# A four-layer decoder on one core: the last width attention and the int8 feed forward, run as two stages or woven into one

## The chip, the cores and the metric

The kernel runs on one core of one Trainium2 chip. The core has five engines that work side by side: TensorE (PE in the profile; its weight loads are shown apart as PEld), VectorE (DVE), ScalarE (ACT), GpSimd (POOL), and SyncE (SP), which here only issues DMAs. Each engine carries out its own instructions strictly in the order of its own program, and waits at a semaphore where it needs something from another engine. The metric is the time of one execution on the device in microseconds (us), the median of several runs.

## The reference, cut to what matters

The whole computation is a decoder of four layers of three blocks on `x`, 16 sequences of 128 tokens with 256 features. Each block's output is added to `x`, and the sum is layer-normed. Only the last two blocks of the twelve bear on this change:

```python
def _L3_xattn_ref(q, k, v, gamma):          # 8 heads; attention over the width
    ...
    qk = jnp.einsum('bhdq,bhdl->bhql', qh, kh) * scale
    sm = jax.nn.softmax(qk, axis=-1)
    ret = jnp.einsum('bhql,bhdl->bhdq', sm, vh)
    return gamma * ret.reshape(B, Dv, Lq)

def _L3_ffn_ref(x, W1, B1, W2, B2):
    X1_q, sX1 = quantize_rowwise(X1)        # round(x * 127/absmax of the row)
    W1_q, sW1 = quantize_global(W1)         # round(w * 127/absmax of the matrix)
    X2 = gelu(int8_matmul_dequant_bias(X1_q, W1_q.T, sX1, sW1, B1))
    X2_q, sX2 = quantize_rowwise(X2)
    W2_q, sW2 = quantize_global(W2)
    return int8_matmul_dequant_bias(X2_q, W2_q.T, sX2, sW2, B2)
...
x = _layernorm(x + _L3_xattn_ref(x, ctx_2048, ctx_2048, L3_xattn_gamma), axis=-1)
x = _layernorm(x + _L3_ffn_ref(x, L3_ffn_W1, L3_ffn_B1, L3_ffn_W2, L3_ffn_B2), axis=-1)
return x
```

Every operation of these two blocks works on one sequence at a time, apart from the two maxima over the whole weight matrices. So sequence 0 can be in the feed forward while sequence 4 is still in the attention.

## The kernel before, in words

The kernel holds all of `x` in SBUF as the tile `X` (128 tokens x 16 sequences x 256 features) and runs twelve stages, `s0` to `s11`, over it. Stages 0 to 2 are woven together; from stage 3 on, `run` opens the pools of one stage, traces it, and goes on to the next. The weights of stage n+1 are loaded (function `w11` for stage 11) when stage n begins. The last two stages are these.

**Stage 10, width attention.** `s10` calls `width_attention`, which stage 7 calls too. One `width_unit` is one sequence `b`. It is a generator: each `yield` ends a step. Its steps are: load `eo`, `e1` and `vp` by DMA (the profile prints `e1` as `e`); twice four matmuls of `eo` with `X` into four PSUM banks and four `tensor_reduce` on DVE that take the row maxima into `npad`; four transposes of `npad` and two DVE operations that make `xp`; twice eight matmuls of `e1` with `xp` and four Exp on ACT into `e`; twice eight matmuls of `vp` with `e`, and a copy on ACT into `o`; four transposes of `o`, two DVE reciprocals `rr`, two POOL multiplications into `rw`; four transposes of `rw`, one DVE product `y`, and two POOL additions of `y` to `X`. After every fourth sequence come two or three steps more (`finish_in_turns`): the layer norm of four sequences, whose statistics are made on DVE (`bn_stats`, `bn_aggr`), the power of -1/2 on POOL (`rsqrt`), and the normalisation on DVE; then 16 transposes on PE and two copies on ACT (`load_transposed`) that write `xT`, which stage 11 doesn't read.

The order of the work is written by hand. `rota(units, lags)` goes through turns n = 0, 1, 2, ...; in each it runs, for each lag in the list, one step of unit n - lag. `Ordered` then makes every engine keep this order: an instruction cannot be moved past another on PE, DVE, ACT or POOL. DMAs on SP stand outside this. The PSUM banks are two rings, six of `psA` (helper `ps`) and two of `psB` (helper `pt`); an instruction that writes a bank waits until the previous content of that place in the ring has been read.

**Stage 11, feed forward.** `s11` first quantises both weight matrices: a maximum on DVE, a maximum over the partitions on POOL (`partition_all_reduce`), then three DVE operations. Then it goes through the groups of four sequences: quantise `X` (`quantise`: maximum, reciprocal, two `tensor_scalar` that scale and round to a whole number in f32, then one `tensor_scalar` that takes the rounding constant off and writes bf16: `t11x` and `q11x`), transposes, the copy `xqT`; for each of the four sequences two matrix products into two banks, two DVE operations that scale and add the bias into `h`, one Gelu on ACT, again the quantisation (`am11h`, `s11h`, `t11h`, `q11h`), eight transposes, the copy `hqT`, eight matmuls, one DVE operation `y11`, one POOL addition to `X`. After each group come the layer norm of the four (`finish`) and one store of them. This stage isn't inside `Ordered`: the scheduler of the language places its instructions, and some of them stand between those of stage 10.

Of the kernel before, what the change touches and what calls it, by code (L numbers as in the profile page):

```python
# [12 lines left out]
F32 = mybir.dt.float32  # L13
# [7 lines left out]
NB = 16  # L21
S = 128
D = 256
# [303 lines left out]
class Decoder:  # L327
# [141 lines left out]
    def run(self):  # L469

        nc, tc = self.nc, self.tc
        names = list(self.stages)

        joint = names[:3] == [0, 1, 2]
        weights = self.weights = {}

        def side(n):
            return ("left", "right")[(n + (joint and n > 1)) % 2]

        def open_weights(n):  # L480
            cm = tc.tile_pool(name=f"w{n}", bufs=1, side=side(n))
            pool = cm.__enter__()
            weights[n] = (cm, getattr(self, f"w{n}")(pool))

        def close_weights(n):
            weights.pop(n)[0].__exit__(None, None, None)

        @contextmanager
        def pools(n):
            with (  # L490
                tc.tile_pool(name=f"k{n}", bufs=2, side=side(n)) as wk,
                tc.tile_pool(name=f"psA{n}", bufs=BANKS.get(n, (5, 3))[0], space=PSUM) as self.psA,
                tc.tile_pool(name=f"psB{n}", bufs=BANKS.get(n, (5, 3))[1], space=PSUM) as self.psB,
            ):
                yield wk

        open_weights(names[0])
        for j, n in enumerate(names):
            if joint and n in (1, 2):
                continue  # L500
            for m in names[1:3] if joint and n == 0 else names[j + 1 : j + 2]:
                open_weights(m)
            w = weights[n][1]
            with ExitStack() as later:
                if joint and n == 0:
                    k12 = later.enter_context(tc.tile_pool(name="k12", bufs=1, side="right"))
                with pools(n) as wk:
                    if j == 0:
                        for g in range(NG):
                            self.load_transposed(g)  # L510
                    if joint and n == 0:
                        held = self.s2_begin(k12, weights[2][1])
                        self.s0(wk, w, False, self.s12_early(k12, weights[1][1], held))
                    else:
                        getattr(self, f"s{n}")(wk, w, n == names[-1])
                close_weights(n)
                if joint and n == 0:
                    if len(names) > 3:
                        open_weights(names[3])
                    with (  # L520
                        tc.tile_pool(name="k2", bufs=2, side="left") as wk,
                        tc.tile_pool(name="psA2", bufs=5, space=PSUM) as self.psA,
                        tc.tile_pool(name="psB2", bufs=3, space=PSUM) as self.psB,
                    ):
                        self.s12_late(k12, wk, weights[1][1], held, len(names) == 3)
            if joint and n == 0:
                close_weights(2)
                close_weights(1)
# [1378 lines left out]
        return None  # L1907

    def s10(self, wk, w, last):
        self.width_attention(wk, self.row("s10_gamma"), last)  # L1910

    def width_attention(self, wk, gamma, last):
        nc = self.nc
        npad = [wk.tile([128, 512], F32, name=f"npad7_{n}", bufs=1) for n in range(3)]
        rw = [wk.tile([128, 2, 2, 128], F32, name=f"rw7_{n}", bufs=1) for n in range(3)]
        for t in npad + rw:
            nc.gpsimd.memset(t, 0.0)
        self.nc = Ordered(self.tc, nc)
        rota(
            [self.width_unit(wk, gamma, npad[b % 3], rw[b % 3], b, last) for b in range(NB)],  # L1920
# [1 line left out]
        )  # L1922
        self.nc = nc

    def width_unit(self, wk, gamma, npad, rw, b, last):
        nc = self.nc
        scale = 0.25
        eo = wk.tile([128, 2, D], F32, tag="eo7", name="eo7", bufs=3)
        e1 = wk.tile([128, 2, D], F32, tag="e17", name="e17", bufs=4)
        vp = wk.tile([128, 2, 8, 32], F32, tag="vp7", name="vp7", bufs=5)  # L1930
        cs = slice(b * 512, b * 512 + 512)
        nc.sync.dma_start(eo.rearrange("p r n -> p (r n)"), self.a["ctx_eo"][:, cs])
        nc.sync.dma_start(e1.rearrange("p r n -> p (r n)"), self.a["ctx_e1"][:, cs])
        nc.sync.dma_start(vp.rearrange("p k h d -> p (k h d)"), self.a["ctx_vp"][:, cs])
        yield
        xb = self.X[:, b, :]

        for mc in range(2):
# [11 lines left out]
        for r in range(2):  # L1950
            for mc in range(2):
                lo = 256 * r + 128 * mc
                nc.tensor.transpose(pm[:, r, mc, :], npad[:, lo : lo + 128], self.ident)
        xp = wk.tile([128, 2, D], F32, tag="xp7", name="xp7", bufs=3)
        for r in range(2):
            nc.vector.scalar_tensor_tensor(
                xp[:, r, :], xb, self.parity[:, r : r + 1],
                pm[:, r].rearrange("p m t -> p (m t)"), ALU.mult, ALU.add,
            )
        yield  # L1960
        e = wk.tile([128, 2, 4, 2, D], F32, tag="e7", name="e7", bufs=3)
        for n in range(2):
            banks = [self.ps(2, D) for _ in range(4)]
            for par in range(2):
# [8 lines left out]
        for par in range(2):  # L1973
# [4 lines left out]
                    )  # L1978
            if par == 0:
                yield  # L1980
        o = wk.tile([128, 2, D], F32, tag="o7", name="o7", bufs=3)
        nc.scalar.copy(o, p)
        yield
        p = self.pt(2, 2, 128)
# [16 lines left out]
        nc.vector.tensor_tensor(y, o, p.rearrange("p r m t -> p r (m t)"), ALU.mult)  # L2001
        for par in range(2):
            nc.gpsimd.tensor_tensor(xb, xb, y[:, par, :], ALU.add)
        if b % 4 == 3:
            yield
            yield from self.finish_in_turns(b // 4, last)

# [358 lines left out]
        nc.sync.dma_start(w["w2"], self.a["s11_w2"].rearrange("(c p) d -> p c d", p=128))  # L2366
        return w

    def s11(self, wk, w, last):
        nc = self.nc  # L2370
        wq, sw = {}, {}
        for n in ("w1", "w2"):
            src = w[n].rearrange("p a b -> p (a b)")
            am = wk.tile([128, 1], F32, name=f"am_{n}", bufs=1)
            nc.vector.tensor_reduce(am, src, AX.X, ALU.max, apply_absolute_value=True)
            al = wk.tile([128, 1], F32, name=f"al_{n}", bufs=1)
            nc.gpsimd.partition_all_reduce(al, am, 128, bass_isa.ReduceOp.max)
            s = wk.tile([128, 1], F32, name=f"s_{n}", bufs=1)
            nc.vector.reciprocal(s, al)
            nc.vector.tensor_scalar(s, s, 127.0, None, ALU.mult)  # L2380
            nc.vector.tensor_scalar(src, src, s, MAGIC, ALU.mult, ALU.add)
            q = wk.tile(list(w[n].shape), BF16, name=f"q_{n}", bufs=1)
            nc.vector.tensor_scalar(q, w[n], MAGIC, None, ALU.subtract)
            nc.vector.tensor_scalar(al, al, 1.0 / (127.0 * 127.0), None, ALU.mult)
            wq[n], sw[n] = q, al
        for g in range(NG):
            xq, am, _ = self.quantise(wk, self.X[:, 4 * g : 4 * g + 4, :], "11x")
            c1 = self.sm(4, tag="c111")
            nc.vector.tensor_scalar(c1, am, sw["w1"], None, ALU.mult)
            p = self.pt(2, 4, 128, dtype=BF16)  # L2390
            for j in range(4):
                for k in range(2):
                    nc.tensor.transpose(p[:, k, j, :], xq[:, j, 128 * k : 128 * k + 128], self.identb)
            xqT = wk.tile([128, 2, 4, 128], BF16, tag="xqT11", name="xqT11")
            nc.scalar.copy(xqT, p)
            for j in range(4):
                b = 4 * g + j
                h = wk.tile([128, 1, 1024], F32, tag="h11", name="h11")
                for n in range(2):
                    p = self.ps(512)  # L2400
                    for k in range(2):
                        self.mm(p, xqT[:, k, j, :], wq["w1"][:, k, 512 * n : 512 * n + 512], k, 2)
                    nc.vector.scalar_tensor_tensor(  # L2403
                        h[:, 0, 512 * n : 512 * n + 512], p, c1[:, j : j + 1],
                        self.row("s11_b1")[:, 512 * n : 512 * n + 512], ALU.mult, ALU.add,
                    )
                nc.scalar.activation(h, h, AF.Gelu_apprx_tanh)
                hq, am2, _ = self.quantise(wk, h, "11h")
                c2 = self.sm(1, tag="c211")
                nc.vector.tensor_scalar(c2, am2, sw["w2"], None, ALU.mult)  # L2410
                p = self.pt(8, 128, dtype=BF16)
                for k in range(8):
                    nc.tensor.transpose(p[:, k, :], hq[:, 0, 128 * k : 128 * k + 128], self.identb)
                hqT = wk.tile([128, 8, 128], BF16, tag="hqT11", name="hqT11")
                nc.scalar.copy(hqT, p)
                p = self.pt(D)
                for k in range(8):
                    self.mm(p, hqT[:, k, :], wq["w2"][:, k, :], k, 8)
                y = wk.tile([128, D], F32, tag="y11", name="y11")
                nc.vector.scalar_tensor_tensor(y, p, c2, self.row("s11_b2"), ALU.mult, ALU.add)  # L2420
                nc.gpsimd.tensor_tensor(self.X[:, b, :], self.X[:, b, :], y, ALU.add)
            self.finish(g, last)


def build(nc, arrays, at, stages):
# [15 lines left out]
```

## Time and profile before

| what | value |
|---|---|
| time, median of 3 runs | 4012.65 us (4009.0 to 4018.32) |
| time of the profiled execution | 4012.83 us |
| its span in the profile | 4011.1 us |
| first reduction of stage 10 (`npad`) on DVE | at 3705.72 us |
| last reduction of stage 10 | ends about 3853 us |
| first `h` of stage 11 on DVE | at 3885.56 us |
| last normalisation | starts at 4005.59 us, 1.38 us |
| DVE, PE, ACT, POOL busy over the whole span | 64%, 90%, 50%, 46% |

The span is counted from the first to the last instruction of the profiled execution; the 1.7 us between it and that execution's time lie outside. A profile line of a group of instructions reads: line of the kernel, engine, operation, what is written `<-` what is read, shapes, how often, then busy time in all and the mean of one in ns, then how long the engine sat idle just before them, and whom it waited for. L324 is the line in `Ordered` through which all the ordered instructions pass, so those are told apart by the names of their tiles. Shares over the whole span say little here: the change concerns the last 310 us.

### The profile page before, as it was taken

The page shows a single profiled execution, that of the slowest core. Times are in us where ns is not written, and L with a number is a line of the kernel's source. Part 1 is how long each engine was busy: PE and PEld are TensorE (multiplying, and loading weights), DVE is VectorE, ACT ScalarE, POOL GpSimd, SP SyncE. Part 2 cuts the span into 40 slices and gives each one's busy share as a digit, 9 for nine tenths or more (in the row PEclk, how much of TensorE's full clock was granted, in tenths as well). Part 3 has the DMA queues.
Part 4 walks back from the last instruction along what each step waited for, and adds up shares of the span by engine and source line. Part 5 has one row for each costly group of instructions (what it writes and reads, how often), then busy time and mean ns, then how long its engine had stood idle before and what let it go on. Part 6 is the DMA issues. An engine that isn't in the chain of part 4 may idle for free.

```text
span 4011.1 us, 96349 instructions
## 1 busy us (share of the span) xinstructions
PE 3606.3 (90%) x39250; PEld 2181.4 (54%) x39250; DVE 2572.9 (64%) x5611; ACT 2012.7 (50%) x4523; POOL 1829.3 (46%) x2013
## 2 busy tenths in 40 slices
PE   6999999999999738798989989888999999998975
PEld 4666666666665425574546655564454554554543
DVE  3776767768767565483245557656667666675786
ACT  2666666666666413352135535325565665664442
POOL 1444444435435227641145532216776666666221
PEclk7999999999999958899989989889999999999986
DMA  2111111111111001100100022101111111112200
GB/s 86 35 38 37 36 39 39 36 33 41 37 33 33 28 16 38 44 2 15 40 30 27 30 85 83 47 1 57 38 39 41 39 38 40 37 41 70 80 17 21
DMA packets 120649, 156.47 MB, mean 39 GB/s; under 512 B 15440, under 2 KB 79696, under 8 KB 119824
## 3 DMA queue, kind: packets, MB, share of 16 engines
q1 hardware_dynamic: 114352, 143.59, 11.5%
q8 instruction: 311, 5.10, 0.5%
q10 hardware_dynamic: 5712, 5.19, 0.4%
q0 software_dynamic: 144, 1.52, 0.1%
q14 instruction: 130, 1.06, 0.1%
HBM read 131.64 MB, written 2.10 MB: 33 GB/s over the span
## 4 chain that ended last, share of the span: by engine, by line
PE 76%; DVE 11%; ACT 5%; POOL 4%; issue 2%; DMA 1%; SPq 0%; ACTq 0%; POOLq 0%; DVEq 0%
PE bankA L324 40%; PE bankB L324 20%; PE bankC L324 8%; PE bankA L465 4%; PE bankB L465 4%; ACT accq L324 1%; DVE X L324 1%; ACT ot L324 1%; ACT gT L324 1%; POOL var L324 1%; DVE npad L324 1%; DVE accq L324 0%; POOL t L324 0%; DVE ln_st L324 0%; DVE h L2403 0%
## 5 line engine op out<-in xcount | busy, mean ns | idle before, releaser
L324 PE MATMUL bankA<-xT,wzx 128*128 128x512 f32 x1024 | 457.7, 600 | 0.0
L324 DVE SCALAR_TENSOR_TENSOR acc<-bankA,half,acc 128x508 f32<-128x508 f32 (+2 forms) x384 | 285.2, 743 | 166.8 <-ACT acc L324 157.8
L324 POOL TENSOR_TENSOR m<-m,gm 128x512 f32<-128x512 f32 x256 | 317.9, 1277 | 45.3 <-ACT m L324 45.3
L324 PEld LDWEIGHTS bankA<-xT,wzx 128*128 128x128 f32 x1024 | 189.8, 190 | 226.5 <-issue 188.3
L324 POOL TENSOR_TENSOR gT<-yx,sz 128x512 f32<-128x512 f32 x128 | 160.6, 1276 | 211.4 <-DVE yx L324 211.4
L324 PE MATMUL bankA<-xT,wkq 128*128 128x512 f32 x512 | 256.5, 625 | 0.0
L324 POOL TENSOR_TENSOR eb<-eb,c_tri_s 128x512 f32<-128x512 f32 x64 | 81.2, 1269 | 372.8 <-ACT eb L324 372.8
L324 PE MATMUL bankA<-xT,wvg 128*128 128x512 f32 x512 | 249.2, 609 | 0.1
L324 ACT ACTIVATE e<-bankA 128x512 f32<-128x512 f32 x320 | 165.2, 603 | 160.7 <-PE bankA L324 160.6
L324 DVE TENSOR_REDUCE npad<-bankA 128x2 f32<-128x512 f32 (+1 forms) x320 | 198.3, 683 | 59.1 <-PE bankA L324 58.8
L324 PE MATMUL bankC<-gT,wo 128*128 128x512 f32 x512 | 233.4, 599 | 2.7 <-POOL gT L324 2.7
L324 ACT ACTIVATE m<-bankA 128x512 f32<-128x512 f32 x256 | 132.1, 604 | 157.4 <-PE bankA L324 157.4
L324 POOL TENSOR_TENSOR sq<-sq,s 128x512 f32<-128x512 f32 x124 | 157.6, 1271 | 56.6 <-ACT s L324 51.9
L324 POOL TENSOR_SCALAR rs_ve<-o_mv 128x4 f32<-128x4 f32 x64 | 31.5, 492 | 299.0 <-DVE o_mv L324 289.7
L324 DVE SCALAR_TENSOR_TENSOR vT<-th,accv 128x512 f32<-128x512 f32 x64 | 45.3, 708 | 182.9 <-ACT th L324 182.9
L324 PEld LDWEIGHTS bankB<-y,tt 32*32 32x32 f32 x8192 | 86.7, 106 | 126.6 <-issue 90.2
L324 DVE SCALAR_TENSOR_TENSOR yx<-xs,cols,bankB 128x512 f32<-128x512 f32 x128 | 94.9, 747 | 90.2 <-PE bankB L324 84.5
L324 DVE SCALAR_TENSOR_TENSOR acck<-bankA,half_cols,acck 128x508 f32<-128x508 f32 (+2 forms) x192 | 142.5, 742 | 13.3 <-ACT acck L324 6.8
L324 PEld LDWEIGHTS bankC<-gT,wo 128*128 128x128 f32 x512 | 93.8, 192 | 99.3 <-issue 94.4
L324 DVE SCALAR_TENSOR_TENSOR accq<-bankA,half_cols,accq 128x508 f32<-128x508 f32 (+2 forms) x192 | 142.1, 740 | 4.5
L324 DVE SCALAR_TENSOR_TENSOR accv<-bankA,half_cols,accv 128x508 f32<-128x508 f32 (+2 forms) x192 | 140.0, 729 | 4.5
L324 ACT ACTIVATE m<-m 128x512 f32<-128x512 f32 x256 | 141.3, 650 | 0.0
(525 smaller groups left out, 9241.9 us busy)
## 6 DMA issues: line engine op xcount, KB each, us to landing
wzx<-in_s_wzx SPq DMA_DIRECT2D x64, 512.0 KB
up<-cums SPq DMA_DIRECT2D x1152, 2.0 KB
wkq<-in_s_w SPq DMA_DIRECT2D x64, 256.0 KB
wvg<-in_s_w SPq DMA_DIRECT2D x64, 256.0 KB
wo<-in_s_wo SPq DMA_DIRECT2D x64, 128.0 KB
sw<-qraw SPq DMA_DIRECT2D x64, 128.0 KB
eo<-in_ctx_eo SPq DMA_DIRECT2D x32, 256.0 KB
e<-in_ctx_e SPq DMA_DIRECT2D x32, 256.0 KB
```

The costliest lines, as they stand in the source:

```text
L324: return lambda *a, **k: self.tc.keep_in_program_order(f(*a, **k))
L465: self.nc.tensor.matmul(out, lhsT=lhsT, rhs=rhs, start=(k == 0), stop=(k == n - 1))
```

## The change

`s10` now traces both blocks. For each sequence there is a pair of generators: `width_unit` (A) without the layer norm at its end, and `s11_unit` (B), which starts with the layer norm of its sequence, does the feed forward of this one sequence, and ends with its second layer norm and the store of one sequence. `weave(units, order)` is the rota for pairs: in turn n each entry (A, lag) or (B, lag) runs one step of that generator of sequence n - lag. All of it is inside `Ordered`. `s11` does nothing more. Stages 0 to 9 issue the same instructions on every engine in the same order as before.

Besides, per sequence: the removal of the rounding constant (`q11x`, `q11h`), both factors `c111`, `c211` and both normalisations of `X` move from DVE to POOL; so does the last operation on the weights (`q_1`, `q_2`). The layer norms and the quantisation of `X` are done for one sequence at a time instead of four. The transposes into `xT` at the end of the attention are gone. `npad` and `rw` have one buffer each instead of three, and `eo`, `e1`, `vp`, `xp`, `e`, `o` have 2, 3, 4, 2, 2, 1 instead of 3, 4, 5, 3, 3, 3. The weights are quantised in four pieces (`first`), one at the start of the second step of each of the first four sequences. ACT now goes from Exp to Gelu and back in each turn in which both blocks are at work; the program has 25 table loads on ACT in this stage, where it had one.

```diff
     def s10(self, wk, w, last):
-        self.width_attention(wk, self.row("s10_gamma"), last)
+        if last:
+            return self.width_attention(wk, self.row("s10_gamma"), last)
+        nc = self.nc
+        npad, rw = self.width_zeros(wk, 1, 1)
+        _, w11 = self.weights[11]
+        with self.tc.tile_pool(name="kk11", bufs=2, side=self.side(11)) as wk11:
+            self.nc = Ordered(self.tc, nc)
+            first = self.s11_weights(wk11, w11)
+            units = [
+                (
+                    self.width_unit(
+                        wk, self.row("s10_gamma"), npad[b % len(npad)], rw[b % len(rw)], b, None,
+                        [2, 3, 4, 2, 2, 1], first,
+                    ),
+                    self.s11_unit(wk11, w11, b),
+                )
+                for b in range(NB)
+            ]
+            A, B = 0, 1
+            weave(units, [
+                (A, 1), (A, 4), (A, 0), (B, 9), (A, 1), (B, 6), (A, 3), (B, 9), (A, 3), (B, 7), (B, 5),
+                (A, 2), (A, 1), (B, 4), (A, 3), (B, 6), (B, 7), (B, 5), (A, 1), (B, 5), (B, 4),
+            ])
+            self.nc = nc
...
+    def s11_weights(self, wk, w):
...
+            nc.vector.tensor_reduce(am, flat, AX.X, ALU.max, apply_absolute_value=True)
+            al = w["s" + n] = wk.tile([128, 1], F32, name=f"al_{n}", bufs=1)
+            nc.gpsimd.partition_all_reduce(al, am, 128, bass_isa.ReduceOp.max)
+            yield
...
+            nc.vector.tensor_scalar(flat, flat, s, MAGIC, ALU.mult, ALU.add)
...
+            nc.gpsimd.tensor_scalar(q, src, MAGIC, None, ALU.subtract)
+            yield
...
+    def layernorm(self, b):
+        xb = self.X[:, b, :]
+        mv, rstd = self.moments([xb], 1e-5, "ln")
+        yield
+        self.nc.gpsimd.tensor_scalar(xb, xb, mv[:, 0, 0:1], rstd[:, 0:1], ALU.subtract, ALU.mult)
+
+    def quantise_row(self, wk, src, m, tag, bufs):
+        nc = self.nc
+        am, s = self.sm(1, tag="am" + tag), self.sm(1, tag="s" + tag)
+        nc.vector.tensor_reduce(am, src, AX.X, ALU.max, apply_absolute_value=True)
+        nc.vector.reciprocal(s, am)
+        nc.vector.tensor_scalar(s, s, 127.0, None, ALU.mult)
+        t = wk.tile([128, m], F32, tag="t" + tag, name="t" + tag)
+        nc.vector.tensor_scalar(t, src, s, MAGIC, ALU.mult, ALU.add)
+        q = wk.tile([128, m], BF16, tag="q" + tag, name="q" + tag, bufs=bufs)
+        nc.gpsimd.tensor_scalar(q, t, MAGIC, None, ALU.subtract)
+        return q, am
+
+    def s11_unit(self, wk, w, b, norm=True):
+        nc = self.nc
+        xb = self.X[:, b, :]
+        if norm:
+            yield from self.layernorm(b)
+            yield
+        xq, am = self.quantise_row(wk, xb, D, "11x", 1)
+        c1 = self.sm(1, tag="c111")
+        nc.gpsimd.tensor_scalar(c1, am, w["s1"], None, ALU.mult)
+        yield
+        p = self.pt(2, 128, dtype=BF16)
+        for k in range(2):
+            nc.tensor.transpose(p[:, k, :], xq[:, 128 * k : 128 * k + 128], self.identb)
+        xqT = wk.tile([128, 2, 128], BF16, tag="xqT11", name="xqT11", bufs=1)
+        nc.scalar.copy(xqT, p)
+        yield
+        h = wk.tile([128, 1024], F32, tag="h11", name="h11", bufs=2)
+        for n in range(2):
...
+            for k in range(2):
+                self.mm(p, xqT[:, k, :], w["q1"][:, k, cs], k, 2)
+            nc.vector.scalar_tensor_tensor(h[:, cs], p, c1, self.row("s11_b1")[:, cs], ALU.mult, ALU.add)
+        yield
+        nc.scalar.activation(h, h, AF.Gelu_apprx_tanh)
+        yield
+        hq, am2 = self.quantise_row(wk, h, 1024, "11h", 1)
+        c2 = self.sm(1, tag="c211")
+        nc.gpsimd.tensor_scalar(c2, am2, w["s2"], None, ALU.mult)
+        yield
+        p = self.pt(8, 128, dtype=BF16)
+        for k in range(8):
+            nc.tensor.transpose(p[:, k, :], hq[:, 128 * k : 128 * k + 128], self.identb)
...
+        nc.scalar.copy(hqT, p)
+        yield
+        p = self.pt(D)
+        for k in range(8):
+            self.mm(p, hqT[:, k, :], w["q2"][:, k, :], k, 8)
+        y = wk.tile([128, D], F32, tag="y11", name="y11")
+        nc.vector.scalar_tensor_tensor(y, p, c2, self.row("s11_b2"), ALU.mult, ALU.add)
+        nc.gpsimd.tensor_tensor(xb, xb, y, ALU.add)
+        yield
+        yield from self.layernorm(b)
+        nc.sync.dma_start(self.out[b], xb)
```

Written out, sequence b has its attention in turns b to b+4 (load; both halves of `npad`, `xp` and the first Exp; the second Exp; `o`, `rr`, `rw`; `y`), its first layer norm in turn b+4, `xqT` and `h` in b+5, Gelu and the quantisation of `h` in b+6, `hqT` and `y11` in b+7, and its last layer norm and the store in b+9. In a turn in which all sequences are there, DVE has in this order: four `npad`, `y`, statistics (of sequence n-9), four `npad`, the quantisation of `X` (n-5), two `xp`, statistics (n-4), two `rr`, the quantisation of `h` (n-6), `y11`, two `h`. POOL has: two additions of `y`, `rsqrt` and the normalisation (n-9), `q11x`, `rsqrt` (n-4), two `rw`, `q11h`, the addition of `y11`, the normalisation (n-4), and the two small factors.

## The prediction

> **What bounds the kernel now.** I read the table of stretches first, because the page's 90% for PE is a mean over twelve stages. Columns: busy us (and instructions) of PE, PEld, DVE, ACT, POOL, then the granted PE clock and the DMA share.
>
> ```profile
> 3740.00:3760.00 20.00, 20.00 (x218) 11.27 (x219) 15.63 (x30) 9.76 (x19) 6.00 (x9) 1.00 0.26 82
> ...
> 3880.00:3900.00 20.00, 9.24 (x44) 4.82 (x42) 19.78 (x43) 8.40 (x8) 0.72 (x1) 0.67 0.00 0
> 3900.00:3920.00 20.00, 13.82 (x63) 7.63 (x64) 15.94 (x46) 3.94 (x5) 4.14 (x5) 0.55 0.06 21
> 3920.00:3940.00 20.00, 9.99 (x58) 6.31 (x56) 16.47 (x39) 6.30 (x7) 2.93 (x3) 0.62 0.02 6
> ```
>
> Stage 10 (first line) has PE full at clock 1.00 and DVE at 78%. Stage 11 has DVE at 80 to 99%, PE half empty at clock 0.55 to 0.67, POOL nearly idle. From the first `npad` (3705.72) to the end (4011.1) pass 305.4 us. The groups of this part give what one sequence costs (busy us, then mean ns of one):
>
> ```profile
> L324 DVE TENSOR_REDUCE npad<-bankA 128x2 f32<-128x512 f32 x128 | 79.3, 683 | 20.1 <-PE bankA L324 20.1
> ...
> L2403 DVE SCALAR_TENSOR_TENSOR h<-bankA,c,rows 128x512 f32<-128x512 f32 x32 | 22.4, 743 | 0.0
> ...
> L2028 DVE TENSOR_REDUCE am11h<-h 128x1 f32<-128x1024 f32 x16 | 19.0, 1210 | 0.1
> ...
> L2034 DVE TENSOR_SCALAR t11h<-h,s11h 128x1024 f32<-128x1024 f32 x16 | 11.9, 744 | 0.0
> L2035 DVE TENSOR_SCALAR q11h<-t11h 128x1024 bf16<-128x1024 f32 x16 | 11.3, 707 | 0.0
> ```
>
> The reader is to see that the idle time before stage 11's DVE groups is nil: DVE sets its pace. In the timeline the first `npad` of successive sequences start at 3705.72, 3713.59, 3722.37, 3730.68 and 3739.82, so a turn of stage 10 takes 8.8 us.
>
> **The change, part by part.** The two stages have different bounds, so woven work can overlap; the question is what one turn with both blocks then costs on each engine.
>
> *DVE, one sequence.* Attention: two groups of four `npad` at 2.48 (timeline), two `xp` 0.87, two `rr` 0.28, `y` 0.69: 6.80. Feed forward: two times statistics (0.42 and 0.17) 1.18; `X` quantised: maximum 0.42 (stage 4's 128x256 reduction), reciprocal 0.15, scale 0.15, `t11x` 0.34; `h` quantised: 1.21, 0.15, 0.15, 0.74; `h` 2 x 0.74 = 1.48; `y11` 0.48: 6.45. Sum **13.25 us**. Gone to POOL are `q11h` 0.71, `q11x` 0.28, two factors and two normalisations at 0.41 to 0.43, some 2 us a sequence.
>
> *POOL.* Two additions 1.54; two `rsqrt` for one column each: 0.23 plus the power, 0.75 for two columns and 1.05 for four, so about 0.60 for one (estimate): 1.7; `rw` 1.18; addition of `y11` 0.72; two factors at 0.25. Two normalisations 128x256 with two operations: nearest row `od` at 1.15, so 2.3. The subtraction, one operation, is bounded by stage 5's `d`, shown below: 0.69 for 256 columns, 3.45 for 1280, so 2.7 ns a column: `q11x` 0.69, `q11h` 2.8. No row has POOL writing bf16, so `q11h` may lie between 2.8 and four times the 1.15 of `od`, 4.6; I take 2.8, the same operation. Sum **11.4** (13.2 with 4.6).
>
> *ACT.* Eight Exp (2.07 for four) 4.14, `o` 0.59, `xqT` 0.37, Gelu 1.06, `hqT` 1.01; two table loads at 1.28: 2.57. Sum **9.7**. The loads are priced by this place, where the next activation follows at once:
>
> ```profile
> 2691.38 1.06 ACT L2133 ACTIVATE parts<-parts 128x1024 f32<-128x1024 f32 x1 [3.54 <-DVE parts L2132]
> 2692.45 1.28 ACT L2134 ACT_TABLE_LOAD   x1
> 2693.74 1.06 ACT L2134 ACTIVATE parts<-parts 128x1024 f32<-128x1024 f32 x1
> ```
>
> The Trainium skill, page "ScalarE: Activation LUTs", section "What ACT_TABLE_LOAD costs", adds a drain of 1.38 us to each load, 2.66 us a switch, which speaks against a program that switches twice a turn; by it ACT would come to 12.5 us a turn. The three rows above show no such drain, since 0.01 us lies on either side.
>
> *PE.* The attention fills its 8.8 us at clock 1.00. The feed forward, from the timeline at clock 0.62: eight transposes 1.06, eight matmuls 1.89, four products 1.38 (5.52 for 16), two transposes 0.27: 4.6, so 2.9 at full clock. Sum **11.7** at clock 1.00, 13.4 if the feed forward's part stays slow.
>
> So DVE is the bound of a full turn. Three things come on top. First, DVE and POOL block each other (POOL's timeline, then DVE's, at the start of stage 5):
>
> ```profile
> 1834.73 3.45 POOL L1644 TENSOR_SCALAR d<-d5i 128x1280 f32<-128x1280 int32 x1 [3.33 <-PE bankB L324]
> 1838.16 2.19 POOL L1645 TENSOR_SCALAR d<-d5i 64x256 f32<-64x256 int32 x1
> ```
> ```profile
> 1836.61 3.05 DVE L1642 TENSOR_SCALAR gu<-gu5i 128x2816 f32<-128x2816 int32 x1
> ```
>
> `gu` ends at 1839.66; had it run from 1838.18, when the first `d` ended, it took 1.5; the second `d` then ran from 1839.66 to 1840.35, 0.69. Each stood still while the other ran. Other DVE work isn't touched: four `npad` take 2.48 beside POOL's additions (from 3748.59; POOL busy from 3747.95 to 3749.49) as they do alone (3743.97). In a full turn DVE has four `tensor_scalar` (`s11x`, `t11x`, `s11h`, `t11h`), and POOL is busy 11.4 of some 15 us. By program order the first two meet the end of a normalisation, the last two the two `rw` of 0.59: 0.1 + 0.6, I take **0.7**; the ends are 0 and 3.3 (each pair behind a normalisation, 1.15, and half an `rw`, 0.5). The Trainium skill, page "SBUF — State Buffer", section "Who interferes with whom", says that a DVE instruction with at most one SBUF input and no two-port mode doesn't contend; by it `npad`, `xp`, `y` and `h` stay free and only those four count. If all DVE work counted, the turn would be up to 13.25 + 11.4 = 24.7 us.
>
> Second, the last part of a turn is a chain over engines: `rr` frees the bank for the transposes of `q11x`, then `xqT`, then eight matmuls 1.15, four products 0.9, then `h`. From `rr` to `h` that is 0.2 + 0.5 + 1.2 + 0.9 = 2.8. Beside it DVE has the quantisation of `h` and `y11`, 2.73. So it is just covered; I take **0.3**, and 0 to 1 as its ends. Third, hand-overs and a PE clock below 1.00: PE with 11.7 of 15 us is like stage 8, where it is 84% busy at clock 0.87; its chain links grow by 0.15. I take **0.7**, between 0 and 1.5. Full turn: 13.25 + 0.7 + 0.3 + 0.7 = **15.0 us**, ends 13.3 and 17.8 (not all at their worst).
>
> *The sum.* Turns 1 to 4, attention alone: 34.1 as now (3739.82 - 3705.72), plus on DVE the second weight's maximum 2.28, both scalings 2 x 1.28 and small ones 0.3: 39.3. (The first maximum, 2.28, lies in DVE's idle time ahead of 3705.72; `q_1` and `q_2`, about 5.6 each by 2.7 ns a column, lie where POOL has nothing else, as do the idle 5.6 us ahead of the first `partition_all_reduce`. If that cover were gone, the first `y` would wait some 3 us.) Turn 5: 6.80 + one statistics 0.6 + 1.06 + `h` 1.48, plus 2.5 of the chain from `rr`, now bare: 12.4. Turn 6: 6.80 + 0.6 + 1.06 + 2.25 + 1.48 + 0.5 = 12.7; turns 7 and 8 with `y11`: 13.2 each. Together 51.5 (45 to 56). Turns 9 to 16 are full: 8 x 15.0 = 120 (106 to 142). Turn 17 lacks `npad` and `xp` (5.83): 9.2, near the 8.8 of a chain-bound turn; turn 18 about 9. From the last `y` to the end, one sequence's chain alone: `y` 0.7, additions 1.5, statistics and `rsqrt` 1.5, normalisation 1.2, quantisation 1.1, `q11x` 0.7, transposes and copy 0.7, products 1.4, `h` 1.5, Gelu 1.1, quantisation 2.3, `q11h` 2.8, transposes 1.1, copy 1.0, matmuls 1.9, `y11` 0.5, addition 0.7, statistics and `rsqrt` 1.5, normalisation 1.2 = 24.4, some 22 hand-overs at 0.1 (3898.69 to 3898.78 from `y11` to POOL) 2.2, behind two other sequences 3 (0 to 8), and store and end as now, 4011.1 - 4006.97 = 4.1: 33.7. In all 39.3 + 51.5 + 120 + 18.2 + 33.7 = 262.7 against 305.4: **42.7 us less**, span 3968.4, and with the 1.7 us outside it **3970 us**. The profiled execution (4012.83) is 0.2 above the median of the runs, which I neglect. SP: each turn's store stands ahead of the next `eo`, but that `eo` is used two turns later, about 20 us, so it costs nothing; the load of 768 KB a turn is what stage 10 does in 8.8 us.
>
> **The rivals.**
> 1. *POOL and DVE shut each other out.* For: POOL's share goes from 4 to 30% in the stretches above to three quarters (11.4 of 15), and `d` and `gu` stood still for each other. Against: only four DVE operations a turn are of that kind. It decides from the point where the four together wait over 0.7 + 43/12 = 4.3 us a turn (12 turns have both blocks), over 1 us each: then the kernel is **slower**. If `t11x` meets `q11h` (2.8) and the rest a normalisation or an addition, 6 us a turn, it is 3970 + 12 x 5.3 = 4034.
> 2. *Nothing overlaps.* If in-order waits lay the blocks end to end, a turn is 8.8 + 8.5 (stage 11 now: about 136 us for 16), and the sum stays at about 4010. Against: in stage 11 the waits are DVE's own length.
> 3. *ACT sets the pace.* If a switch costs twice the row, ACT has 12.3 us, and Exp of the second half of a sequence waits for the load behind `hqT`; 1.5 us a turn more: 3970 + 12 x 1.5 = 3988.
> 4. *The order isn't what it says:* the instruction lists of each engine show it woven, so next to no chance.
>
> **How the numbers follow.** Forecast (turn 13.3 to 17.8, times 3946 to 4000) 0.74; ACT 0.10; no overlap 0.06; lock, slower 0.10. Adding the ends of the parts, 39 + 45 + 106 + 17 + 30 gives 3944; 41 + 56 + 142 + 20 + 39 gives 4005. The range is 3944 to 4005. A measurement tells 0.2%, 8 us, from no change: faster (below 4004.6) 0.84, same 0.06, slower 0.10.
>
> **What would show it.** Right: in the profile after, turns (from one group of four `npad` to the same of the next sequence) of about 15 us, DVE busy near 90% in turns 9 to 16, POOL three quarters, PE clock above 0.8, no ACT wait ahead of Exp over 1 us. Wrong: `t11x` or `t11h` far over 0.74; `q11h` over 4 us; DVE idle for PE or POOL by over 2 us a turn; a tail after the last `npad` over 60 us.

## The result and the profile after

The changed kernel takes **3959.41 us**, the median of 3 runs (3959.33 to 3960.51), against 4012.65 us before: a ratio of 0.9867, interval [0.9844, 0.9889], 53 us less. Its profiled execution took 3960.51 us, with a span of 3958.7 us. From the first `npad` (3703.43) to the end it has 255.3 us, where the kernel before has 305.4.

Below, this stretch from the first `npad` to the end is called **the last part**, and the kernels are compared by it where a few us matter: the stages ahead of it, which no kernel here changes, end at different moments from execution to execution (the first `npad` of the profiled executions starts between 3698.72 and 3711.58), which moves the times of one kernel by 10 to 20 us (before: 4005 to 4025 over all its runs here) and is left out of the last part.

First the stretches, with the same columns as before (PE, PEld, DVE, ACT, POOL, PE clock, DMA share):

```profile
3840.00:3860.00 20.00, 19.05 (x192) 10.68 (x192) 19.69 (x43) 14.54 (x21) 18.97 (x24) 1.00 0.16 54
3880.00:3900.00 20.00, 15.07 (x179) 9.34 (x178) 16.75 (x42) 15.59 (x23) 18.86 (x25) 1.00 0.03 9
3900.00:3920.00 20.00, 11.65 (x80) 6.22 (x80) 11.28 (x25) 5.93 (x8) 19.05 (x25) 0.71 0.04 13
3920.00:3940.00 20.00, 10.23 (x44) 4.74 (x44) 12.08 (x27) 3.87 (x6) 18.94 (x22) 0.50 0.04 14
```

In the full turns (first line) PE, DVE and POOL are all busy for some 95% or more and the PE clock is 1.00: the reader sees three engines nearly full at once, where before there was one at a time. From 3900 on POOL alone is full; DVE has 11 to 12 of 20 us and PE's clock falls to 0.50. Now the groups of the last part, that answer to those shown before (busy us, mean ns, then the idle time ahead of them):

```profile
L324 DVE TENSOR_REDUCE npad<-bankA 128x2 f32<-128x512 f32 x128 | 78.8, 681 | 5.8 <-PE bankA L324 5.7
...
L324 POOL TENSOR_SCALAR q11h<-t11h 128x1024 bf16<-128x1024 f32 x16 | 44.4, 2775 | 2.0 <-DVE t11h L324 0.8
...
L324 POOL TENSOR_SCALAR rw<-rr,rows 128x128 f32<-128x128 f32 x32 | 24.2, 767 | 7.8 <-DVE npad L324 7.8
L324 DVE SCALAR_TENSOR_TENSOR h<-bankA,c,rows 128x512 f32<-128x512 f32 x32 | 22.8, 741 | 9.8 <-PE bankA L324 8.2 <-POOL rw L324 1.5
...
L324 DVE TENSOR_REDUCE am11h<-h 128x1 f32<-128x1024 f32 x16 | 18.8, 1175 | 0.6 <-ACT h L324 0.6
...
L324 DVE TENSOR_SCALAR t11h<-h,s11h 128x1024 f32<-128x1024 f32 x16 | 13.3, 832 | 0.6
```

`npad`, `h` and `am11h` take what they took before (681, 741, 1175 against 683, 743, 1210 ns). `q11h` on POOL takes 2775 ns where DVE took 707. `t11h` has become longer, 832 against 744, and `rw` too, 767 against 604. The idle time ahead of `npad` has gone from 20.1 to 5.8 us: DVE hardly waits any more.

Two views show where the time of a turn goes. The first is the timeline of one full turn, which begins with `npad` at 3841.25 and ends at 3853.89 (12.64 us); here its POOL `rw` and `q11h`, and DVE's `t11h` and `y11`:

```profile
3851.10 1.64 POOL L324 TENSOR_SCALAR rw<-rr,rows 128x128 f32<-128x128 f32 x2
...
3851.40 0.86 DVE L324 TENSOR_SCALAR t11h<-h,s11h 128x1024 f32<-128x1024 f32 x1
...
3852.18 0.47 DVE L324 SCALAR_TENSOR_TENSOR y<-bankB,c,rows 128x256 f32<-128x256 f32 x1
...
3852.82 2.77 POOL L324 TENSOR_SCALAR q11h<-t11h 128x1024 bf16<-128x1024 f32 x1
```

`rw` and `t11h` are there at the same time, and both are longer than alone: the pair of `rw` 1.64 instead of 1.18, `t11h` 0.86 instead of 0.74. And `y11` starts at 3852.18, though `t11h` is shown until 3852.26: on a full engine an instruction starts before the one ahead of it has ended. The second view is the chain of waits of the tail, in order of time:

```profile
3903.29 2.77 POOL q11h L324
3906.34 2.60 POOL X L324 x3
...
3912.12 1.19 POOL q11x L324
...
3914.54 1.21 POOL rw L324 x2
3915.84 2.77 POOL q11h L324
...
3932.32 0.43 DVE am11x L324
...
3948.42 1.90 PE bankB L324 x8
```

Up to 3932 it is POOL nearly throughout, and the same instruction comes back after 12.55 us (`q11h` at 3903.29 and 3915.84): DVE has no `npad` left in these turns, and they are as long as the full ones. From 3932.32 to the end, 26.4 us, the chain is that of the last sequence alone, over DVE, POOL, PE and ACT in turn.

### The profile page after: what moved, and what is told of

The parts are those of the page before. It is cut to its first block, busy times and chain, and to the rows that moved or that the text cites. A ratio compares the mean times of both kernels' runs of the same rounds, so it can differ in the third digit from the quotient of the medians.

```text
span 3958.7 us, 96423 instructions
## 1 busy us (share of the span) xinstructions
PE 3577.9 (90%) x39218; PEld 2165.0 (55%) x39218; DVE 2553.5 (65%) x5561; ACT 2040.0 (52%) x4551; POOL 1963.1 (50%) x2155
## 4 chain that ended last, share of the span: by engine, by line
PE 74%; DVE 12%; POOL 5%; ACT 5%; issue 2%; DMA 1%; SPq 0%; ACTq 0%; POOLq 0%; DVEq 0%
PE bankA L324 39%; PE bankB L324 19%; PE bankC L324 8%; PE bankA L465 4%; PE bankB L465 3%; DVE npad L324 2%; ACT accq L324 1%; ACT ot L324 1%; ACT gT L324 1%; POOL var L324 1%; DVE X L324 1%; DVE ln_st L324 1%; DVE accq L324 1%; POOL X L324 1%; POOL t L324 1%
## 5 line engine op out<-in xcount | busy, mean ns | idle before, releaser
L324 POOL TENSOR_SCALAR rs_ve<-o_mv 128x4 f32<-128x4 f32 x64 | 31.4, 491 | 299.2 <-DVE o_mv L324 289.8
L324 ACT ACTIVATE acc<-bankA,half 128x512 f32<-128x512 f32 x128 | 100.5, 785 | 79.6 <-PE bankA L324 79.6
```

Source lines behind the costliest of these rows:

```text
L324: return lambda *a, **k: self.tc.keep_in_program_order(f(*a, **k))
```

## The experiments

All numbers of the table are from the profiled execution of each kernel: the last part, the full turn (mean of seven, from the `xp` of the 9th sequence to that of the 16th), and the tail from that last `xp` to the end. Time and ratio are those of the timed runs; each ratio is to the runs of the kernel before that were made along with it, and their medians lie between 4012.65 and 4015.72. In the ramp ahead of the full turns, the stretch from the first `xp` to the fourth takes between 31.4 and 34.5 us in the woven kernels, which have the same instructions there, so a difference of 3 us in the last part is not told from none.

| kernel | last part | full turn | tail | time (median) | ratio to before |
|---|---|---|---|---|---|
| before | 305.4 | - | - | 4012.65 | 1 |
| changed | 255.3 | 12.61 | 72.5 | 3959.41 | 0.9867 [0.9844, 0.9889] |
| pieces without weave | 368.6 | - | - | 4074.67 | 1.0142 [1.0125, 1.0158] |
| before, no `xT` | 303.1 | - | - | 4015.27 | 0.9996 [0.9986, 1.0005] |
| Tanh for Gelu | 257.7 | 12.62 | 72.5 | 3964.91 | 0.9871 [0.9848, 0.9894] |
| `q11h` twice | 298.8 | 15.57 | 89.5 | 4005.14 | 0.9972 [0.9960, 0.9985] |
| subtractions on DVE | 249.4 | 13.57 | 56.5 | 3960.34 | 0.9859 [0.9841, 0.9876] |
| tail on DVE | 247.7 | 12.62 | 65.5 | 3954.16 | 0.9853 [0.9832, 0.9874] |
| `t11h` on ACT | 280.3 | 15.09 | 71.5 | 3982.71 | 0.9923 [0.9904, 0.9942] |
| `q11h` on ACT | 292.2 | 17.05 | 63.1 | 3995.25 | 0.9956 [0.9943, 0.9970] |
| both on ACT | 298.9 | 17.11 | 69.4 | 4007.20 | 0.9978 [0.9968, 0.9989] |
| `q11h` late on ACT | 242.7 | 12.52 | 60.4 | 3949.41 | 0.9840 [0.9823, 0.9856] |
| that, and tail on DVE | 244.1 | 12.52 | 62.3 | 3953.55 | 0.9848 [0.9831, 0.9864] |
| both late on ACT, tail on DVE | 242.9 | 12.24 | 63.2 | 3953.39 | 0.9849 [0.9833, 0.9864] |

**Is the gain the overlap?** The same pieces, the attention (with the number of buffers that the kernel before has) and then the feed forward, each kept in order by `Ordered`:

```diff
-        if last:
-            return self.width_attention(wk, self.row("s10_gamma"), last)
+        return self.width_attention(wk, self.row("s10_gamma"), None)
...
-        if 10 in self.stages:
-            return
...
-        for b in range(NB):
-            for _ in self.s11_unit(wk, w, b, False):
-                pass
+        rota(
+            [self.s11_unit(wk, w, b) for b in range(NB)],
+            [5, 2, 5, 3, 1, 0, 2, 3, 1, 1, 0],
+        )
```

> The new pieces without the weave: all sixteen attention units first (rotated as before), then all sixteen feed-forward units in a rotation of their own, with the same POOL share, the same single statistics and stores. Theory (the gain is the overlap of the two blocks): attention alone takes some 150 us from the first npad, the feed forward then has POOL as its bound at 8.7 us a turn, 16 x 8.7 = 140 and a ramp of some 25, so 315 against 255 us in the changed kernel: 4010 to 4040 us, not faster than before. Rival (the gain comes from the pieces: no turned copy of X, work spread over POOL): at or below 3985 us.

It is 1.0142 [1.0125, 1.0158] of before: the pieces without the weave are 63 us worse (368.6 against 305.4), the weave then takes 113 us off (255.3). So the direction is shown, and the rival is dead; the size was expected too small. The last part divides into 158.6 us of attention, 37.5 us from its last addition on POOL (ends at 3860.31) to the first `rsqrt` of the feed forward (3897.81) in which little but the weights is worked on, and 172.5 us of feed forward. The 37.5 us I had hardly counted: they are bare here, and are covered for the most part by the first four turns in the changed kernel, which take 40.4 us where the kernel before takes 34.1. And POOL's turn is 10.14 us, not 8.7. One reason, which makes up 0.5 of these 1.4 us, stands in its timeline, POOL's first and then DVE's:

```profile
3945.11 0.86 POOL L324 TENSOR_SCALAR q11x<-t11x 128x256 bf16<-128x256 f32 x1
3945.96 0.84 POOL L324 TENSOR_SCALAR c<-am11x,al 128x1 f32<-128x1 f32 x1
```
```profile
3945.99 0.76 DVE L324 TENSOR_SCALAR t11h<-h,s11h 128x1024 f32<-128x1024 f32 x1
```

The factor `c` for one column takes 0.84 us here and 0.30 in the changed kernel: it ends 0.05 us after `t11h` on DVE ends.

**Is it the unneeded `xT`?** The kernel before, with the call changed so that stage 10 does not make it:

```diff
-            yield from self.finish_in_turns(b // 4, last)
+            yield from self.finish_in_turns(b // 4, last, gamma is self.ones)
```

> The kernel before, without the turned copy of X (xT) that the end of stage 10 makes and that stage 11 does not read; the changed kernel leaves it out too. Theory: it stands in four of sixteen turns, each some 1.5 to 2 us longer for it, so 6 to 10 of the 53 us: 4003 to 4007 us. Rival (most of the gain is this leftover): 3985 us or less.

The ratio is 0.9996 [0.9986, 1.0005], the last part 2.3 us shorter. The rival is dead, and my own 6 to 10 us were too many. From the first `xp` to the sixteenth it gains 4.0 us (138.8 against 142.8): two turns of 10.80 and 10.65 us become 8.73, but the other long ones stay at 10.3 to 10.4, and those have the four statistics, or the four normalisations and stage 11's maximum over `X`, in them.

**Does ACT matter?** Gelu gives way to Tanh:

```diff
-        nc.scalar.activation(h, h, AF.Gelu_apprx_tanh)
+        nc.scalar.activation(h, h, AF.Tanh)
```

> The changed kernel with Tanh in the place of Gelu, which changes that part of the computation; Tanh and Exp need no table load between them if the number of loads falls from 25. Theory (the loads are covered by DVE's and POOL's work): 0 to 3 us less than the changed kernel, 3956 to 3960 us. Rival (ACT's switches hold up Exp and so the turn): 12 turns at 1.5 us or more, 3941 us or less.

No table load is left between Exp and Tanh in the full turns, and the turn is 12.62 us, as before it: the loads were covered entirely. The last part is 2.4 us longer, all of it in the ramp, and the ratio, 0.9871, is not told from the changed kernel's 0.9867.

**Is POOL full?** `q11h` is computed twice:

```diff
-        nc.gpsimd.tensor_scalar(q, t, MAGIC, None, ALU.subtract)
+        for _ in range(1 + (m == 1024)):
+            nc.gpsimd.tensor_scalar(q, t, MAGIC, None, ALU.subtract)
```

> The changed kernel with q11h computed twice on POOL from the same t11h. Theory (POOL is at 12.5 us a turn, level with DVE, and the bound of the tail): each of the 16 turns gets 2.8 us longer, so a turn of 15.3 us in the middle and 16 x 2.8 = 45 us in all: 4000 to 4005 us. Rival (POOL has 1 us or more to spare in a full turn, DVE alone sets it): 2 us or less a turn in the middle, 3990 us or less.

POOL's timeline, where each line is both of them:

```profile
3840.06 5.63 POOL L324 TENSOR_SCALAR q11h<-t11h 128x1024 bf16<-128x1024 f32 x2
...
3855.39 5.63 POOL L324 TENSOR_SCALAR q11h<-t11h 128x1024 bf16<-128x1024 f32 x2
...
3871.02 5.63 POOL L324 TENSOR_SCALAR q11h<-t11h 128x1024 bf16<-128x1024 f32 x2
```

They come 15.33 and 15.63 us apart; the mean turn is 15.57 instead of 12.61, 2.96 more for 2.8 us of work, and the last part 43.5 us longer. (From `xp` to `xp` these turns go to and fro between 14.4 and 16.5 us; why stays open.) So POOL has nothing to spare in a full turn, and the rival, DVE alone, is dead.

**Is DVE full too?** The subtraction of `quantise_row` goes back to it:

```diff
-        nc.gpsimd.tensor_scalar(q, t, MAGIC, None, ALU.subtract)
+        nc.vector.tensor_scalar(q, t, MAGIC, None, ALU.subtract)
```

> The changed kernel with both subtractions (q11x, q11h) back on DVE, where the kernel before had them. Theory (DVE and POOL are both full in the full turns, POOL alone in the tail): DVE gets 0.2 + 0.6 us more a turn by the distances at which it starts such instructions, so a full turn of 13.3 to 13.5 us and 12 x 0.8 = 10 us more; POOL falls to 8.9 us a turn, which makes the tail 10 to 14 us shorter: 3953 to 3960 us. Rival (only POOL is full in the full turns): turns below 12.4 us there, 3945 us or less.

Its stretches, a full one and one of the tail:

```profile
3840.00:3860.00 20.00, 18.45 (x153) 10.32 (x154) 19.52 (x42) 14.49 (x21) 13.63 (x19) 1.00 0.22 75
...
3900.00:3920.00 20.00, 13.10 (x116) 8.31 (x114) 18.46 (x48) 11.25 (x16) 19.05 (x30) 0.86 0.04 14
```

DVE has 19.5 of 20 us in the full turns and POOL only 13.6, and the turn is 13.57: 0.96 longer for what DVE took over (0.70 for `q11h` and 0.29 for `q11x`; its busy time in a turn goes from 12.34 to 13.23). The tail is 16 us shorter. With the kernel ahead, both limits are shown: in the full turns DVE and POOL are both full, in the tail POOL is so alone. PE, also near 95% in the changed kernel, was not tried by itself, but the chain of waits of the full turns (3841 to 3866) has no piece of PE in it. The move of the subtractions to POOL, taken by itself, gains 10 us up to the last `xp` (3.5 in the ramp and 6.7 in the seven full turns) and loses 16 at the end (249.4 against 255.3 in the last part). The times, 3960.34 and 3959.41 us, do not tell the two kernels apart.

**The tail alone.** From turn 17 on, the subtractions and the normalisations are on DVE:

```diff
+    def turn(self, b, lag):
+        return self.nc.vector if b + lag > 16 else self.nc.gpsimd
...
-        nc.gpsimd.tensor_scalar(q, t, MAGIC, None, ALU.subtract)
+        eng.tensor_scalar(q, t, MAGIC, None, ALU.subtract)
```

> The changed kernel, but from turn 17 on, where no attention is left, the subtractions (q11x, q11h) and the normalisations run on DVE instead of POOL. Theory (the tail is 15 us longer than predicted since POOL, at 12.55 us a turn, is its bound): POOL falls to about 3 us a turn and DVE rises to 7.5, so turns 17 to 19 take 8.5 to 9 us instead of 12.55, and the last sequence's chain loses 2.1 for q11h and 0.8 for a normalisation: 10 to 15 us less than the changed kernel, 3944 to 3950 us. Rival (the tail is the chain over all engines at a low PE clock): 4 us less at most, 3955 us or more.

7 us off the tail (65.5 against 72.5), between the theory and the rival. Moving the subtractions alone took 16 off: from `y` to `y`, turns 17 and 18 took 8.5 and 8.9 us there and take 13.9 and 10.7 here. With the normalisations on DVE too, DVE carries nearly all of the work, and in its order each turn has it waiting for POOL's `ln_rs` ahead of the normalisation, first 5.2 us (at 3895.25), then 1.9 (10.7 us from one to the next, at 3905.95 and 3916.63).

**The idle engine, first try.** Three kernels put `t11h`, `q11h` or both on ACT, in the place where they stood:

```diff
+            nc.scalar.activation(t, src, AF.Identity, scale=s, bias=self.magic[:, 0:1])
...
+            nc.scalar.activation(q, t, AF.Identity, bias=self.magic[:, 1:2])
```

> The changed kernel with t11h on ACT (Identity, the same scale and offset) instead of DVE. Theory (in a full turn DVE and POOL are both full, POOL at 12.5 us with 0.5 us of it standing still in rw while t11h runs): DVE falls by 0.75 us a turn, but the turn only by what POOL gets back, 0.3 to 0.5 us: 3 to 6 us less than the changed kernel, 3953 to 3957 us, and rw back near 604 ns. Rival (DVE alone sets the full turn): 12 x 0.75 = 9 us less, 3950 us or less.

> The changed kernel with q11h on ACT (Identity with the offset) instead of POOL. Theory (both full in the middle, POOL alone in the tail): POOL falls to 9.7 us a turn, the full turns stay at 12.5 to 12.6 us since DVE still fills them, and the tail gets 8 to 12 us shorter: 3947 to 3952 us. Rival (POOL sets the full turn and DVE only looks full): full turns of 12.0 us or less, 3942 us or less.

> The changed kernel with t11h and q11h both on ACT. Theory: DVE then has about 11.8 us a turn, POOL 9.3, ACT 9.7 + 2 x 1.06 = 11.8, PE 11.5: a full turn of 12.0 to 12.3 us, 4 to 7 us less for twelve of them, and the tail 8 to 12 us shorter: 3941 to 3948 us. Rival (ACT, now full, with two table loads a turn, holds up Exp): a turn of 13 us or more, 3960 us or more.

All three theories missed: full turns of 15.09, 17.05 and 17.11 us. The rivals of the first two missed as well. That of the third has the right numbers (13 us or more, 3960 or more) but not the reason, for ACT is far from full: in the four stretches from 3800 to 3880 it is busy for 11.9 to 15.7 of 20 us. The timeline of the kernel with `q11h` on ACT, all engines, in order of time:

```profile
3841.02 0.79 DVE L324 TENSOR_SCALAR t11h<-h,s11h 128x1024 f32<-128x1024 f32 x1
...
3841.90 1.15 ACT L324 ACTIVATE q11h<-t11h,magic 128x1024 bf16<-128x1024 f32 x1 [1.20 <-DVE t11h L324]
...
3842.95 0.35 ACT L324 COPY xqT<-bankB 128x256 bf16<-128x256 bf16 x1
...
3843.20 2.06 ACT L324 ACTIVATE e<-bankA 128x512 f32<-128x512 f32 x4
...
3843.59 0.81 PE L324 MATMUL bankA<-q,xqT 128*128 128x512 bf16 x3 [2.50 <-ACT xqT L324]
```

ACT has to take `q11h` ahead of `xqT` and of the second four Exp; `q11h` waits for `t11h`, which is near the end of DVE's turn; `xqT` follows it, and PE stands still for 2.50 us until `xqT` is there, with the products of the next `npad` behind it in its queue. So DVE gets its next work late, and with it the next `t11h`: a ring over ACT, PE and DVE that is 17 us long. In the other two kernels ACT waits in the same place for `s11h`, 0.4 to 0.7 us; with `t11h` alone the turns go between 13.9 and 16.7 us, and why they alternate stays open. The reading of the ring is tried in the next kernel; that `t11h` alone has the same cause is not shown.

**The idle engine, in another place.** `q11h` is a step of its own, behind the second four Exp:

```diff
-                (A, 2), (A, 1), (B, 4), (A, 3), (B, 6), (B, 7), (B, 5), (A, 1), (B, 5), (B, 4),
+                (A, 2), (A, 1), (B, 4), (A, 3), (B, 6), (B, 7), (B, 5), (A, 1), (B, 6), (B, 5), (B, 4),
```

> The changed kernel with q11h on ACT again, now as a piece of its own behind the xqT and the second four Exp of its turn instead of ahead of them. Theory (it was the place in ACT's queue that made the turns 17 us: xqT and Exp stood behind a wait for t11h): full turns of 12.5 to 12.7 us, set by DVE, and a tail 8 to 12 us shorter, as POOL falls to 9.7 us a turn: 3947 to 3952 us. Rival (ACT has no room for it wherever it stands): turns of 13.5 us or more, 3970 us or more.

ACT's timeline, and the stretch around it:

```profile
3845.79 0.40 ACT L324 COPY xqT<-bankB 128x256 bf16<-128x256 bf16 x1
3846.65 2.06 ACT L324 ACTIVATE e<-bankA 128x512 f32<-128x512 f32 x4 [0.46 <-PE bankA L324]
3848.57 1.17 ACT L324 ACTIVATE q11h<-t11h,magic 128x1024 bf16<-128x1024 f32 x1
3849.76 1.28 ACT L324 ACT_TABLE_LOAD   x1
3851.06 1.06 ACT L324 ACTIVATE h<-h 128x1024 f32<-128x1024 f32 x1
```
```profile
3840.00:3860.00 20.00, 17.97 (x194) 10.98 (x184) 19.48 (x48) 16.67 (x25) 15.89 (x25) 1.00 0.28 91
```

`xqT` and Exp go first, `q11h` waits for nothing, and the turn is 12.52: the same instruction on the same engine, 4.5 us a turn apart. That shows the place to be the cause. POOL has 15.9 of 20 us now, and the turn is shorter by only 0.09: DVE, with 19.5, holds it. The tail is 12 us shorter. By its times (3943.16 to 3952.73) this kernel lies below every run of the changed one; the intervals of the two ratios overlap a little.

**Further on that way.** With the tail on DVE besides, and then with `t11h` on ACT too, just ahead of `q11h` (the first kernel has only the last of the two `else` lines):

```diff
+        if b + 6 > 16:
+            nc.vector.tensor_scalar(hq, t, MAGIC, None, ALU.subtract)
+        else:
+            nc.scalar.activation(t, h, AF.Identity, scale=s, bias=self.magic[:, 0:1])
+            nc.scalar.activation(hq, t, AF.Identity, bias=self.magic[:, 1:2])
```

> The kernel with q11h on ACT behind the second four Exp, and from turn 17 on both subtractions and the normalisations on DVE. Theory: the full turns stay at 12.5 us (DVE), the tail is that of the kernel whose tail was moved to DVE, entered a little sooner since POOL is not late: 3944 to 3950 us. Rival (POOL's lateness at the end of the full turns costs nothing): the same as that kernel, 3950 to 3954 us.

> As the kernel with q11h late on ACT and the tail on DVE, and t11h on ACT too, just ahead of q11h. Theory: DVE falls to about 11.8 us a turn, POOL is at 9.3, ACT at 9.7 + 1.24 + 1.15 = 12.1, PE at 11.5, so a turn of 12.1 to 12.4 us, 2 to 6 us less than with t11h on DVE: 3940 to 3947 us. Rival (ACT, nearly full, holds up Gelu and Exp): a turn of 12.8 us or more, 3953 us or more.

The first is no gain over the kernel ahead (244.1 against 242.7). Its tail is 3.1 us shorter than that of the kernel with the tail alone on DVE (62.3 against 65.5), so POOL's lateness at the end of the full turns was worth some 3 us and not what most of the tail is made of. The second brings the turn to 12.24, as expected, but its last part (242.9) is only 1.2 us shorter than the first's, which is not told from none, and its time, 3953.39 us, is not the 3940 to 3947 of the theory. One stretch of the second:

```profile
3840.00:3860.00 20.00, 18.54 (x172) 11.02 (x167) 18.83 (x47) 19.29 (x29) 15.23 (x24) 1.00 0.29 93
```

ACT, DVE and PE are now at 19.3, 18.8 and 18.5 of 20 us, so little is left in the full turns in this order of work. The middle of this kernel (12.24 a turn) with the tail of the one that has only the subtractions on DVE (56.5) would have a last part of some 236 us, an estimate from those two rows; it was not run.

## Why the prediction was right, point by point

| part | predicted | measured |
|---|---|---|
| turns 1 to 4 | 39.3 | 40.4 |
| turns 5 to 8 | 51.5 | 47.1 |
| turns 9 to 16 | 120 | 100.9 |
| turns 17 and 18 | 18.2 | 25.3 |
| from the last `y` to the end | 33.7 | 41.6 |
| sum | 262.7 | 255.3 |

The marks are the first `npad` of turns 1, 5 and 9 (3703.43, 3743.88, 3790.93), the attention's `y` of turns 17 and 19 (3891.80, 3917.13), and the end. The total was 7 us too high because larger errors of opposite sign partly cancelled: up to turn 16 the parts are 22.4 us shorter than forecast, from turn 17 on 15.0 longer. So the mechanism held (the work of the two blocks overlaps, and DVE sets the pace of a full turn), but that the time fell well inside its range is in part luck: the full turn, 12.61 us, lies below the lower end, 13.3, that the forecast gave it. The rest of the distance from 3970 to 3959.41 lies outside the last part: its first `npad` came 2.3 us sooner, and the median is 1.1 below the profiled execution.

1. *DVE bounds a full turn: right, with company.* The lines of DVE's timeline of one turn (from 3841.25) add up to 13.22 us; I had 13.25. The additions to it were wrong. I put 1.7 us on top, and the turn is 0.6 *below* the sum, since here, on an engine without gaps, most instructions start 0.06 to 0.10 us before the one ahead of them ends (those that read the result of the one ahead start some 0.03 us after its end, as `s11h` at 3851.01 behind `am11h`, 3849.81 for 1.17). The timeline of before shows the same (`y` at 3853.82 for 0.69 us, `xp` at 3854.43). The kernel with the subtractions on DVE shows that it is DVE that counts: 0.89 us more busy time there, 0.96 us more a turn.
2. *The lock: right in kind, but on the other side.* DVE loses about 0.18 us a turn (`t11h` 0.86, `t11x` 0.40 against 0.34), not 0.7; POOL loses 0.46 in `rw`. Rival 1 needed 4.3 us a turn. With `t11h` off DVE in the last kernel, `rw` is back at 620 ns a piece (836 in the full turns of the changed kernel, 840 with only `q11h` late on ACT), which shows the cause. `npad`, `xp`, `y` and `h` are no longer than before. The Trainium skill, page "SBUF — State Buffer", section "Who interferes with whom", says that where a DVE instruction is in a two-port mode, whichever of the two engines issues first keeps the shared pair of ports for its whole instruction and the other is fully blocked. `c` at 0.84 us beside a `t11h` of 0.76 agrees with the blocking; it does not settle which goes first, for `c` is shown to start 0.03 us ahead of `t11h` and yet waits.
3. *The chain from `rr` to `h` (0.3) and the hand-overs (0.7): nearly nothing.* In the chain of waits of the full turns every piece is DVE's but for pauses of 0.02 to 0.31 us, and PE's clock is 1.00, not 0.87.
4. *POOL: 11.4 predicted, 12.15 by the lines of its timeline of one turn.* `q11h` is 2.8, as taken from `d`. `q11x` is 0.86, not 0.69: 0.86 for 256 columns and 2.77 for 1024 make 2.5 ns a column and a fixed 0.2 us. The rest is the lock (0.46) and the two factors, 0.30 each instead of 0.25. So POOL, which I had at three quarters, was full (83.4 of 88.3 us in the seven full turns), and doubling `q11h` showed it.
5. *The tail: the step that failed.* "Turn 17 lacks `npad` and `xp` (5.83): 9.2" looked at DVE alone. POOL keeps all its work in turns 17 and 18, and my own sum of it, 11.4, was already above 9.2. They took 25.3 instead of 18.2. The end took 7.9 more, since POOL was still behind: the term "behind two other sequences 3 (0 to 8)" was some 10, an estimate (the last quantisation of `X` starts at 3932.32, 15.2 us after the last `y`, and the steps between add up to some 5.4 by the prediction's own terms). The sign "a tail after the last `npad` over 60 us" did come true (73.6 us, from 3885.16). The kernel with the tail on DVE gives turns of 13.9 and 10.7 us, that with the subtractions alone there 8.5 and 8.9.
6. *ACT: right.* Eight Exp, two copies, Gelu and two loads of 1.28 are hidden; without the loads the turn is the same. In the rows shown the next activation starts 0.02 us after a load ends (3849.76 + 1.28, then 3851.06). The Trainium skill, page "ScalarE: Activation LUTs", section "What ACT_TABLE_LOAD costs", adds a drain of 1.38 us to each load; these rows don't show it.
7. *Rivals 2 and 3.* No overlap would have been 4074.67 us with these pieces, not 4010. The 8.8 us of a turn of stage 10 that this rival starts from is not the mean of the starts shown beside it, which is 8.5 ((3739.82 - 3705.72) / 4), but later turns take 8.77. ACT does not set the pace in the changed kernel; in the kernel with `q11h` ahead of `xqT` the place in its queue did, though it was far from full.

## What to carry to other kernels

When two stages with different bounds are woven, price the turns in which only one of them is left as carefully as the full ones: an engine that merely keeps up in the middle can bound the end, if its work there doesn't shrink. On an engine without gaps, read the pace from the distance between starts, not from the durations. And before moving an operation to an engine with room, look at what stands behind it in that engine's queue: the same `q11h` cost 4.4 us a turn in one place and nothing in another.

## What the runs showed of the hardware

POOL is shown idle around `partition_all_reduce` without a cause that the profile shows. In the kernel without the weave, where nothing covers it, the first of the two starts 5.5 us after its input `am` is there (3860.89, then 3866.38) and the second 5.8 us after POOL's last instruction (3879.25, then 3885.06), and the subtraction `q` behind each starts 5.4 and 5.2 us after the scaling on DVE that it reads (3868.47, then 3873.85; 3887.15, then 3892.32): 22 of the 37.5 bare us. In the changed kernel the second one starts at 3725.55, and the `rw` behind it only at 3733.75, 4.5 us after the `rr` that it reads (3728.96, 0.27 us): so the weave does not cover all of it. What POOL did in these gaps no run was made to tell.
